# A Mamba layer whose C is broadcast by DMA and copied to PSUM by ScalarE, with pairs of B products in one operation and softplus' correction on ScalarE and TensorE

## The chip, the core and the metric

The kernel runs on one core of a Trainium2 chip, everything in float32. A core has five engines with an instruction queue each, executed in order: TensorE (PE in the profile) for matrix products into PSUM, VectorE (DVE), ScalarE (ACT) for functions of single values, GpSimd (POOL), which reads and writes SBUF only, and SyncE (SP), whose queue here issues DMA transfers. They wait for one another through semaphores. The metric is device time of one execution in microseconds; less is better.

## The reference

Four layers on an image batch x of (2, 128, 56, 56), each `x = x + layer(groupnorm(x))`: agent attention, a 3x3 convolution, a mixture of experts over 2x2 patches, and a pair of Mamba blocks. Only the last one is changed. Its rows are the 112 image rows of 56 points with 128 channels; one Mamba ("f") runs over a row from left to right, the other ("b") from right to left. For each, with inner width 256 and 16 states:

```python
xi, z = jnp.split(x @ in_w.T, 2, axis=-1)
xc = silu(conv_b + sum(xp[:, k:k+L, :] * conv_w[:, k] for k in range(4)))
dt, B, C = split(xc @ xproj_w.T, [8, 8 + 16])
dt = softplus(dt @ dt_w.T + dt_b)
# scan over the 56 points of a row, h of (256, 16):
h = exp(dt * A) * h + (dt * xc) * B
y = (h * C).sum(states)
y = (y + xc * D) * silu(z)
out = y @ out_w.T
```

Both outputs are joined by `fuse_w`, layer-normalized over the channels, and added to x.

## The kernel before, in words

The first three layers fill the time up to about 1710 us; the Mamba layer follows to the end. Each image is cut into 7 blocks of 8 rows, BLK = 448 points, so there are 14 blocks. In a block the two ways follow each other, and a way has 8 pairs of states, each in two units (m = 0 and 1, the two halves of the 256 inner channels): 16 units a way, 32 units a block, 448 in all. A tile of a unit holds 2 states x 64 channels on the 128 partitions and 2 x 448 points along the free axis (the index r takes the other 64 channels of the half).

What one unit needs, with the line in the profile:

- **decay** (L1820): ScalarE writes `dA = exp(dt2 * A)`, two activations of 128x448, into one of two PSUM tiles.
- **push** (L1831): GpSimd multiplies `dtu2` by the pair's row of `Bs` into `dBu`; four buffers.
- **scan** (L1853): VectorE runs the recurrence over 896 points. After the second unit of a pair the 128x1792 tile h is multiplied by C: for the pooled pairs (0, 3, 6 of way f and 0, 3 of way b) by GpSimd from `Cs` (L1859), for the eleven others by VectorE from the PSUM tile `c_ps` (L1862).
- **read_out** (L1841): for those others TensorE writes C into `c_ps`: one row of the low product `lo`, taken with a column of the identity matrix spread over 64 columns, is broadcast to 64 partitions; four matmul instructions a pair.
- **collect** (L1873): TensorE sums h over states into y, some three units behind the scan; **close** (L1879) multiplies y by `zs` on VectorE at a way's end.

What prepares the next way is spread over the units by a hand-written agenda: `book(step, stage)` puts a stage after the unit of that step. A stage mostly issues TensorE's products at once, and its ScalarE part ("fetch") at the next unit, or one later with `late`. The stages: **norm**, **conv** (L1703, L1712), **silu** (two table loads around two Silu), **low** (dt, B and C before their expansion), **send_low** (SP: `lo` to DRAM as `far`, and from there broadcast into `Bs` and, for the pooled pairs alone, into `Cs`), **step** (L1755, L1765 to L1769: dt's product, then |v|, relu(v), e = exp(-|v|) and, back into the PSUM bank, ue = 1 + e), **error** (L1775, VectorE: (ue - 1) - e, the rounding error of ue), **log** (L1780, ScalarE: u = ln(ue)), **softplus** (L1785: TensorE sums u - error + relu over three matrices; L1786 copies dt back), **weigh** (L1793, GpSimd: dt * xc, and a memset of the rows' first points), **send_steps** (L1808, SP: eight transfers that lay dt and dt * xc out as `dt2` and `dtu2`), **gate**. After a block come **fuse**, **measure**, **root**, **newton**, **normalize**, **turn_back** and **onto**.

PSUM is full: two tiles of 1024 for dA, y, one bank under the tag "mm" and one under "c". Stages and `c_ps` share these last two one after the other, so a stage booked with `tag="c"` stands in line with the multiplies by C. All five engines' orders are as the program issues them: for unit n the loop issues decay of unit n + 1, the fetches due, push of unit n + 3, the scan of n, a close that is due, read_out, collects, then the agenda's stages of step n.

Of the kernel before, what the change touches and what calls it, by code (L numbers as in the profile page):

```python
# [17 lines left out]
P = 128  # L18
# [1513 lines left out]
def mamba_pair(net, out, wts, combine):  # L1532
# [19 lines left out]
    with ExitStack() as ctx:  # L1552
# [7 lines left out]
        def gathered(name):  # L1560

            if name == "g0":
                g = work.tile([P, 2, 2, BLK], F32, name=name, tag="h", bufs=4).rearrange("p m r t -> p (m r t)")
            else:
                g = work.tile([P, 2, BLK], F32, name=name, tag="dBu", bufs=4).rearrange("p r t -> p (r t)")
            return g[:T, :512]
# [123 lines left out]
        class Half:  # L1690


            def __init__(self, blk, w):
                self.blk, self.w = blk, w
                self.dA, self.dBu, self.hc = {}, {}, {}
# [20 lines left out]
            def gate(self, m):  # L1716
                pm = mm("gate_ps")
                if m == 0:
                    self.zs = work.tile([P, 2, BLK], F32, name="zs", tag=f"zs{self.w.d}", bufs=1 if self.w.d == "f" else 2)
                nc.tensor.matmul(  # L1720
                    rows(pm[:, :BLK]),
                    self.w.gate[:, m, :],
                    self.blk.xn[:, :, K - 1 : K - 1 + HW],
                    start=True,
                    stop=True,
                )
                return lambda: nc.scalar.copy(self.zs[:, m, :], pm[:, :BLK])
# [9 lines left out]
            def send_low(self):  # L1737

                pooled = self.w.pooled
                far = dram.tile([2 * S, BLK], F32, name="far", tag="far")  # L1740
                nc.sync.dma_start(far, self.lo[R:, :])
                self.B = work.tile([P, PAIRS, BLK], F32, name="Bs", tag="Bs")
                self.C = work.tile([P, len(pooled), BLK], F32, name="Cs", tag=f"Cs{self.w.d}", bufs=1)
                for s in range(2):
# [3 lines left out]
                    for n, j in enumerate(pooled):  # L1748
                        r = S + 2 * j + s
                        nc.sync.dma_start(self.C[half, n, :], far[r : r + 1, :].to_broadcast([H, BLK]))  # L1750


            def step(self, m):
                pm = mm("dt_ps")
                nc.tensor.matmul(pm[:, :BLK], self.w.dt_t[:, m, :], self.lo[:R, :], start=True, stop=True)  # L1755
                if m == 0:
                    self.e = work.tile([P, 2, BLK], F32, name="sp_e", tag="sp_e", bufs=1)
                    self.dt = work.tile([P, 2, BLK], F32, name="dt", tag="dt")
                    self.ue = {}
# [8 lines left out]

# [3 lines left out]

            def error(self, m):
                e = self.e[:, m, :]
                nc.vector.scalar_tensor_tensor(e, self.ue[m], 1.0, e, ALU.subtract, ALU.subtract)  # L1775

            def log(self, m):
                if m == 0:
                    self.u = work.tile([P, 2, BLK], F32, name="sp_u", tag="sp_u", bufs=1)
                nc.scalar.activation(self.u[:, m, :], self.ue[m], AF.Ln)  # L1780

            def softplus(self, m):
                pm = mm("sp_ps")
                for n, (mat, v) in enumerate(((net.ident, self.u), (minus, self.e), (net.ident, self.dt))):
                    nc.tensor.matmul(pm[:, :BLK], mat, v[:, m, :], start=n == 0, stop=n == 2)  # L1785
# [13 lines left out]
            def send_steps(self, m=None):  # L1799

                some = slice(0, 2) if m is None else slice(m, m + 1)
                if not m:
                    self.dt2 = work.tile([P, 2, 2, BLK], F32, name="dt2", tag="dt2")
                    self.dtu2 = work.tile([P, 2, 2, BLK], F32, name="dtu2", tag="dtu2")
# [22 lines left out]
            def push(self, u):  # L1827
                j, m = self.unit(u)
                shape = [P, 2, BLK]
                self.dBu[u] = work.tile(shape, F32, name="dBu", tag="dBu", bufs=4)  # L1830
                nc.gpsimd.tensor_tensor(  # L1831
                    self.dBu[u], self.dtu2[:, m], self.B[:, j, :].unsqueeze(1).to_broadcast(shape), ALU.mult
                )

            def read_out(self, u):

                r = R + S + u // 2 * 2
                self.c_ps = ps.tile([P, 512], F32, name="c_ps", tag="c")
                for s in range(2):
                    one_row = net.ident[:LOW, r + s : r + s + 1].to_broadcast([LOW, H])  # L1840
                    nc.tensor.matmul(self.c_ps[s * H : (s + 1) * H, :BLK], one_row, self.lo, start=True, stop=True)  # L1841

            def scan(self, u):
# [5 lines left out]
                hf, bf = (v.rearrange("p r t -> p (r t)") for v in (h[:, m], self.dBu[u]))  # L1849
# [4 lines left out]
                if m == 1:  # L1854
                    shape = [P, 4, BLK]
                    h4 = h.rearrange("p m r t -> p (m r) t")
                    if self.by_pool(u):
                        c = self.C[:, self.w.pooled.index(j), :].unsqueeze(1).to_broadcast(shape)
# [18 lines left out]
            def close(self):  # L1877
                self.yv = work.tile([P, 2, BLK], F32, name="yv", tag=f"yv{self.w.d}", bufs=1)
# [18 lines left out]
        for n, blk in enumerate(blocks):  # L1897
# [3 lines left out]
            if n == 0:  # L1901
# [9 lines left out]
                for m in range(2):  # L1911
                    book(at + 10 + m, lambda f=f, m=m: f.error(m))
# [9 lines left out]
                for m in range(2):  # L1922
                    book(2 + 3 * m, lambda b=b, m=m: b.step(m))
                    book(3 + 3 * m, lambda b=b, m=m: b.error(m))
# [5 lines left out]
            else:  # L1930
# [11 lines left out]
                book(at + 19, lambda f=f: f.error(0))  # L1942
                book(at + 19, lambda f=f: f.log(0))
                book(at + 20, lambda f=f: f.step(1))
                book(at + 21, lambda f=f: f.error(1))
# [8 lines left out]
                book(at + 28, lambda b=b: b.error(0))  # L1954
                book(at + 28, lambda b=b: b.log(0))
                book(at + 29, lambda b=b: b.step(1))
                book(at + 31, lambda b=b: b.error(1))
# [5 lines left out]
                book(at + 35, lambda b=b: b.gate(0))  # L1963
# [47 lines left out]
        with tc.manual_schedule(engines={E.PE, E.Activation, E.DVE, E.Pool, E.SP}):  # L2011
            units[0][0].decay(0)
            for h, u in units[:3]:
                h.push(u)
            for n, (h, u) in enumerate(units):
# [4 lines left out]
                if n + 3 < len(units):  # L2020
                    who, i = units[n + 3]
                    who.push(i)
# [3 lines left out]
                if u % 2 == 0 and not h.by_pool(u):  # L2026
                    h.read_out(u)
# [115 lines left out]
```

## Time and profile before

| What | us |
|---|---|
| median of 3 runs (lowest, highest) | 3111.37 (3110.33, 3111.38) |
| the profiled execution's own time | 3104.97 |
| its span, first to last instruction | 3103.2 |
| first scan starts, last scan starts | 1736.9, 3073.4 |

| Engine, 1737 to 3070 us (1333 us) | busy us |
|---|---|
| TensorE, matmuls | 1184.50 |
| VectorE | 1247.53 |
| ScalarE | 964.97 |
| GpSimd | 1284.22 |

The profile is one execution. Busy time counts an instruction from start to end, and neighbours on one engine overlap by some tenths of a microsecond, so what an engine can do is read from the distance between starts. A wait is put down to the engine whose semaphore came last. TensorE's clock has two values in the records, full and half; an average clock of 0.89 over a stretch means that it ran at half speed for about a fifth of it.

### The profile page before, as it was taken

How to read it: one execution, taken by the hardware profiler on the slowest of the kernel's cores; microseconds unless marked ns; L12 is line 12 of the kernel's file. 1: busy time of each engine (PE TensorE's matmuls, PEld its weight loads, DVE VectorE, ACT ScalarE, POOL GpSimd, SP SyncE). 2: the span in 40 equal slices, each digit the busy share in tenths (PEclk: the TensorE clock that was granted, in tenths of full speed). 3: DMA queues.
4: the chain of work that ended last, by engine and by line, in shares of the span. 5: the costliest groups of instructions: out<-in, count | busy, mean ns of one | idle time of the engine just before them, and what ended most of it. 6: DMA issues, size and time to landing. Idle time of an engine off the chain costs nothing. (4 is left out here: it accounts for less than half of the span.)

```text
span 3103.2 us, 34608 instructions
## 1 busy us (share of the span) xinstructions
PE 2821.9 (91%) x12964; PEld 1076.6 (35%) x12964; DVE 2224.9 (72%) x2033; ACT 1758.6 (57%) x2634; POOL 1499.1 (48%) x801
## 2 busy tenths in 40 slices
PE   7999999999898899999996789989899998889885
PEld 3333333332334444444443322333323333233321
DVE  5879999999887111111112699999999999999996
ACT  5778788877641011111111577776677767777764
POOL 3000100100511000000003699999999999999995
PEclk9999999999998899999997888999889899999987
DMA  1000000000011878787773553454444535444440
GB/s 54 1 1 1 1 1 1 1 1 1 1 38 43 317 280 323 286 314 301 298 309 104 115 102 81 91 106 90 93 89 84 112 81 113 90 84 91 95 101 8
DMA packets 133271, 333.65 MB, mean 108 GB/s; under 512 B 20228, under 2 KB 90340, under 8 KB 129492
## 3 DMA queue, kind: packets, MB, share of 16 engines
q1 hardware_dynamic: 111104, 303.96, 34.0%
q0 software_dynamic: 5520, 15.62, 1.6%
q10 hardware_dynamic: 16452, 11.61, 1.2%
q8 instruction: 106, 1.74, 0.2%
q14 instruction: 89, 0.73, 0.1%
HBM read 262.56 MB, written 17.20 MB: 90 GB/s over the span
## 5 line engine op out<-in xcount | busy, mean ns | idle before, releaser
L1831 POOL TENSOR_TENSOR dBu<-dtu,Bs 128x896 f32<-128x896 f32 x448 | 943.6, 2136 | 51.7 <-DVE h L1853 39.1
L1853 DVE TENSOR_TENSOR_SCAN h<-dA,dBu 128x896 f32<-128x896 f32 x448 | 878.7, 2006 | 59.7 <-ACT dA L1820 47.4
L620 ACT ACTIVATE ex<-sc 128x896 f32<-128x896 f32 (+1 forms) x700 | 602.7, 917 | 124.4 <-PE sc L617 113.3
L627 DVE TENSOR_TENSOR ex_sum<-ex_sum,ex 128x1792 f32<-128x1792 f32 (+1 forms) x238 | 492.5, 2069 | 35.2 <-ACT ex L620 21.2
L1873 PE MATMUL y<-h,both 128*64 128x448 f32 x1792 | 469.1, 625 | 16.1 <-POOL h L1859 14.9
L617 PE MATMUL sc<-q,k 32*128 32x448 f32 (+1 forms) x2800 | 403.5, 587 | 3.6 <-ACT ex L620 2.9
L1341 PE MATMUL h_ps<-w,xs_c 128*128 128x512 f32 x896 | 393.4, 597 | 10.3 <-issue 10.3
L1820 ACT ACTIVATE dA<-dt,f_A 128x448 f32<-128x448 f32 x448 | 284.4, 637 | 107.0 <-DVE h L1853 76.4
L635 PE MATMUL av<-ex,va 128*32 128x448 f32 (+1 forms) x2800 | 334.3, 552 | 0.1
L1862 DVE TENSOR_TENSOR h<-h,c_ps 128x1792 f32<-128x1792 f32 x154 | 311.3, 2021 | 26.2 <-PE c_ps L1841 11.5
L582 POOL TENSOR_TENSOR a_e<-a_e,a_inv 112x784 f32<-112x784 f32 x14 | 41.6, 2974 | 583.2 <-ACT ex L620 394.5
L1820 ACT ACTIVATE dA<-dt,b_A 128x448 f32<-128x448 f32 x448 | 283.8, 636 | 66.6 <-DVE h L1853 53.2
L1345 DVE TENSOR_TENSOR he<-h_ps,sg 128x512 f32<-128x512 f32 x56 | 38.5, 691 | 381.8 <-PE h_ps L1341 344.3
L1289 POOL DMA_INDIRECT xr<-xd,whom x28 | 28.1, 1003 | 534.8 <-PE xr_ps L1331 490.1
L1859 POOL TENSOR_TENSOR h<-h,Cs 128x1792 f32<-128x1792 f32 x70 | 279.3, 3990 | 2.5 <-DVE h L1853 2.4
L1841 PE MATMUL c_ps<-low,ident 40*64 40x448 f32 x616 | 172.9, 643 | 89.6 <-DVE h L1862 67.5
L1341 PEld LDWEIGHTS h_ps<-w,xs_c 128*128 128x128 f32 x896 | 169.0, 191 | 218.5 <-issue 202.8
L1873 PEld LDWEIGHTS y<-h,both 128*64 128x64 f32 x1792 | 116.7, 150 | 320.0 <-issue 250.7
L617 PEld LDWEIGHTS sc<-q,k 32*128 32x128 f32 (+1 forms) x2800 | 137.7, 181 | 230.0 <-issue 135.2
L1362 PE MATMUL o_ps<-w,ht 128*128 128x512 f32 x448 | 197.2, 592 | 0.4 <-ACT ht L1357 0.4
L1344 ACT ACTIVATE sg<-h_ps 128x512 f32<-128x512 f32 x56 | 33.4, 597 | 256.0 <-PE h_ps L1341 256.0
L1364 ACT ACTIVATE ot<-o_ps,share 128x512 f32<-128x512 f32 x28 | 19.3, 688 | 278.9 <-PE o_ps L1362 278.9
(334 smaller groups left out, 3057.9 us busy)
## 6 DMA issues: line engine op xcount, KB each, us to landing
w<-in_L_conv_w_dram SPq DMA_DIRECT2D x28, 4096.0 KB, 19.4
w<-in_L_conv_w_dram SPq DMA_DIRECT2D x28, 2048.0 KB, 10.2
Bs<-far SPq DMA_DIRECT2D x56, 896.0 KB, 8.6
dtu<-sp_u SPq DMA_DIRECT2D x108, 224.0 KB, 3.9
dt<-dt SPq DMA_DIRECT2D x108, 224.0 KB, 5.2
Cs<-far SPq DMA_DIRECT2D x140, 112.0 KB, 7.3
os<-ot ACTq DMA_DIRECT2D x28, 256.0 KB, 7.8
xd<-xt SPq DMA_DIRECT2D x14, 224.0 KB, 2.7
```

The costliest lines, as they stand in the source:

```text
L617: nc.tensor.matmul(sc[:size, j, :BLK], self.m.k[rows, at : at + size], self.q[rows, :], start=True, stop=True)
L620: nc.scalar.activation(ex[:size, 2 * g : 2 * g + 2, :], sc[:size, :, :BLK], AF.Exp, scale=scale)
L627: nc.vector.tensor_add(self.total[g][:size], self.total[g][:size], ex[:size])
L635: nc.tensor.matmul(self.av[rows, :BLK], self.m.va[:size, i, rows], self.ex[i][:size, h, :], start=i == 0, stop=i == STEPS - 1,)
L1341: nc.tensor.matmul(h_ps, xc[:, q, :], w1[:, q, f0 : f0 + 512], start=q == 0, stop=q == 3)
L1362: nc.tensor.matmul(o_ps, ht[:, i, :], w2[:, i, :], start=i == 0, stop=i == nj - 1)
L1820: nc.scalar.activation(self.dA[u][:, r * BLK : (r + 1) * BLK], self.dt2[:, m, r, :], AF.Exp, scale=self.w.A[:, j, 2 * m + r : 2 * m + r + 1],)
L1831: nc.gpsimd.tensor_tensor(self.dBu[u], self.dtu2[:, m], self.B[:, j, :].unsqueeze(1).to_broadcast(shape), ALU.mult)
L1853: nc.vector.tensor_tensor_scan(hf, af, bf, 0.0, ALU.mult, ALU.add)
L1859: nc.gpsimd.tensor_tensor(h4, h4, c, ALU.mult)
L1862: nc.vector.tensor_tensor(h4, h4, c, ALU.mult)
L1873: nc.tensor.matmul(self.y[r * H : (r + 1) * H, m, :BLK], both, self.hc[j][:, m, r, :], start=False, stop=j == PAIRS - 1)
```

## The change

C now reaches the SBUF for every pair: `send_c` issues two broadcast transfers from `far` a pair, six units ahead, into five buffers. `read_out` becomes a ScalarE copy from there to the PSUM tile and is issued ahead of the scan. `push` makes the products of both units of a pair in one GpSimd operation of 128x1792, two pairs ahead, into three buffers of twice the size. `error` is gone: ScalarE writes ue - 1 into a quarter of `dtu2`, and softplus adds four matrices, e - (ue - 1) + u + relu. `close` writes into `zs`, whose buffers change places (two for f, one for b). A few bookings move.

```diff
             def send_low(self):
-                pooled = self.w.pooled
-                far = dram.tile([2 * S, BLK], F32, name="far", tag="far")
+                far = self.far = dram.tile([2 * S, BLK], F32, name="far", tag="far")
                 nc.sync.dma_start(far, self.lo[R:, :])
                 self.B = work.tile([P, PAIRS, BLK], F32, name="Bs", tag="Bs")
-                self.C = work.tile([P, len(pooled), BLK], F32, name="Cs", tag=f"Cs{self.w.d}", bufs=1)
...
-                    for n, j in enumerate(pooled):
-                        r = S + 2 * j + s
-                        nc.sync.dma_start(self.C[half, n, :], far[r : r + 1, :].to_broadcast([H, BLK]))
+            def send_c(self, j):
+                self.C[j] = work.tile([P, BLK], F32, name="Cs", tag="Cs", bufs=5)
+                for s in range(2):
+                    r = S + 2 * j + s
+                    nc.sync.dma_start(
+                        self.C[j][s * H : (s + 1) * H, :], self.far[r : r + 1, :].to_broadcast([H, BLK])
+                    )
...
-            def error(self, m):
-                e = self.e[:, m, :]
-                nc.vector.scalar_tensor_tensor(e, self.ue[m], 1.0, e, ALU.subtract, ALU.subtract)
             def log(self, m):
...
                 nc.scalar.activation(self.u[:, m, :], self.ue[m], AF.Ln)
+                nc.scalar.activation(self.dtu2[:, m, 0, :], self.ue[m], AF.Identity, bias=-1.0)
             def softplus(self, m):
                 pm = mm("sp_ps")
-                for n, (mat, v) in enumerate(((net.ident, self.u), (minus, self.e), (net.ident, self.dt))):
-                    nc.tensor.matmul(pm[:, :BLK], mat, v[:, m, :], start=n == 0, stop=n == 2)
+                terms = (
+                    (net.ident, self.e[:, m, :]),
+                    (minus, self.dtu2[:, m, 0, :]),
+                    (net.ident, self.u[:, m, :]),
+                    (net.ident, self.dt[:, m, :]),
+                )
+                for n, (mat, v) in enumerate(terms):
+                    nc.tensor.matmul(pm[:, :BLK], mat, v, start=n == 0, stop=n == 3)
...
-            def push(self, u):
-                j, m = self.unit(u)
-                shape = [P, 2, BLK]
-                self.dBu[u] = work.tile(shape, F32, name="dBu", tag="dBu", bufs=4)
+            def push(self, j):
+                shape = [P, 4, BLK]
+                self.dBu[j] = work.tile([P, 2, 2, BLK], F32, name="dBu", tag="dBu", bufs=3)
                 nc.gpsimd.tensor_tensor(
-                    self.dBu[u], self.dtu2[:, m], self.B[:, j, :].unsqueeze(1).to_broadcast(shape), ALU.mult
+                    self.dBu[j].rearrange("p m r t -> p (m r) t"),
+                    self.dtu2.rearrange("p m r t -> p (m r) t"),
+                    self.B[:, j, :].unsqueeze(1).to_broadcast(shape),
+                    ALU.mult,
                 )
             def read_out(self, u):
-                r = R + S + u // 2 * 2
                 self.c_ps = ps.tile([P, 512], F32, name="c_ps", tag="c")
-                for s in range(2):
-                    one_row = net.ident[:LOW, r + s : r + s + 1].to_broadcast([LOW, H])
-                    nc.tensor.matmul(self.c_ps[s * H : (s + 1) * H, :BLK], one_row, self.lo, start=True, stop=True)
+                nc.scalar.copy(self.c_ps[:, :BLK], self.C[u // 2])
...
             def close(self):
-                self.yv = work.tile([P, 2, BLK], F32, name="yv", tag=f"yv{self.w.d}", bufs=1)
+                self.yv = self.zs
...
-                book(at + 28, lambda b=b: b.log(0))
-                book(at + 29, lambda b=b: b.step(1))
-                book(at + 31, lambda b=b: b.error(1))
+                book(at + 29, lambda b=b: b.log(0))
+                book(at + 30, lambda b=b: b.step(1))
                 book(at + 31, lambda b=b: b.log(1))
...
-                book(at + 35, lambda b=b: b.gate(0))
+                book(at + 38, lambda b=b: b.gate(0))
...
+            for h, u in units[:6:2]:
+                h.send_c(u // 2)
             units[0][0].decay(0)
-            for h, u in units[:3]:
-                h.push(u)
+            for h, u in units[:4:2]:
+                h.push(u // 2)
             for n, (h, u) in enumerate(units):
...
                 fetch(n)
-                if n + 3 < len(units):
-                    who, i = units[n + 3]
-                    who.push(i)
+                if u % 2 == 0 and not h.by_pool(u):
+                    h.read_out(u)
+                if u % 2 == 0 and n + 6 < len(units):
+                    who, i = units[n + 6]
+                    who.send_c(i // 2)
+                if n % 2 == 0 and n + 4 < len(units):
+                    who, i = units[n + 4]
+                    who.push(i // 2)
                 h.scan(u)
                 if done:
                     done.pop().close()
-                if u % 2 == 0 and not h.by_pool(u):
-                    h.read_out(u)
                 waiting.append((h, u))
```

Tiles that were written to a `dBu` buffer during the gather before the layer take the new shape, and `dtu2` is made in `step` instead of `send_steps`; all other bookings of `error` are taken out.

## Prediction

> **What bounds the kernel now.** The change lies in the Mamba layer, from the first scan at 1736.9 us to the last at 3073.4. I read the groups of instructions first, for who is full there: the page's groups (line, engine, operation, shapes, count | busy us, mean ns | idle).
>
> ```profile
> L1831 POOL TENSOR_TENSOR dBu<-dtu,Bs 128x896 f32<-128x896 f32 x448 | 943.6, 2136 | 51.7 <-DVE h L1853 39.1
> L1853 DVE TENSOR_TENSOR_SCAN h<-dA,dBu 128x896 f32<-128x896 f32 x448 | 878.7, 2006 | 59.7 <-ACT dA L1820 47.4
> ...
> L1862 DVE TENSOR_TENSOR h<-h,c_ps 128x1792 f32<-128x1792 f32 x154 | 311.3, 2021 | 26.2 <-PE c_ps L1841 11.5
> ...
> L1859 POOL TENSOR_TENSOR h<-h,Cs 128x1792 f32<-128x1792 f32 x70 | 279.3, 3990 | 2.5 <-DVE h L1853 2.4
> ```
>
> VectorE and GpSimd are both nearly full. Who holds whom is in the waits of 1900 to 3060 us, 12 blocks (waiter <- releaser: us, times, longest):
>
> ```profile
> ACT sp_u L1780 <- DMA dtu<-sp_u: 44.9, 12, 4.4
> DVE h L1853 <- ACT dA L1820: 38.8, 35, 2.0
> ...
> ACT dt L1786 <- PE sp_ps L1785: 37.2, 25, 2.5
> ...
> POOL dBu L1831 <- DVE h L1853: 29.3, 34, 1.9
> ...
> DVE h L1862 <- PE c_ps L1841: 5.2, 12, 0.9
> ```
>
> The scan waits for ScalarE's dA, never to speak of for GpSimd's dBu, while GpSimd waits for scans to free its buffers. So the layer's pace is VectorE's own work plus the holes that ScalarE's in-order queue tears in it; GpSimd, however full, follows. The holes of one block, in the timeline of VectorE (start, length, ... [idle before <- releaser]):
>
> ```profile
> 2315.90 3.94 DVE L1853 TENSOR_TENSOR_SCAN h<-dA,dBu 128x896 f32<-128x896 f32 x2 [1.11 <-ACT dA L1820]
> ...
> 2330.89 2.02 DVE L1862 TENSOR_TENSOR h<-h,c_ps 128x1792 f32<-128x1792 f32 x1 [0.66 <-PE c_ps L1841]
> ...
> 2358.25 7.77 DVE L1853 TENSOR_TENSOR_SCAN h<-dA,dBu 128x896 f32<-128x896 f32 x4 [0.84 <-ACT dA L1820]
> ...
> 2378.86 0.61 DVE L1775 SCALAR_TENSOR_TENSOR sp_e<-dt_ps,sp_e 128x448 f32<-128x448 f32 x1
> 2381.46 3.94 DVE L1853 TENSOR_TENSOR_SCAN h<-dA,dBu 128x896 f32<-128x896 f32 x2 [1.98 <-ACT dA L1820]
> ```
>
> A block of 32 units: a scan run of four takes 7.76, so 1.92 from start to start; a pair read out on VectorE is 1.92 + 2.10 + 1.94 = 5.96, a pooled one 3.85; 11 x 5.96 + 5 x 3.85 = 84.8; two yv at 1.0, the layer norm's small operations 1.8, four corrections (L1775) at 0.53 start to start: 90.7. Holes 0.5 (mean) + 0.43 + 0.84 + 1.98 = 3.7. Sum 94.4; measured 95.0 (scans of unit 0 at 2322.42 and seven blocks later at 2987.37). GpSimd in a block: 32 x 2.10 + 5 x 3.96 + 5.5 = 92.5.
>
> **The change, part by part.** Sums are made against the profiled execution, 3105.0 us (span 3103.2); it lies 6.4 under the median 3111.4, which I add at the end.
>
> *B products of a pair.* 16 operations of 128x1792 for 32 of 128x896. The multiply by C on L1859 has exactly that shape and kind: 3.96 start to start. 16 x 3.96 = 63.4 against 67.2: GpSimd -3.8 a block, to 88.7. As the scan hardly waits for it this is worth 0; its upper bound, if GpSimd set the pace, is 3.8 x 14 = 53 us. Behind it: after weigh at step 25 only one push (3.96) stands before the next way's first, where three (6.3) stood; that push waited 0.92 for its data at 2314.20, and will wait some 3.3. It still ends about 3 us ahead of its scan. Cost 0, bound 2.4 a block.
>
> *The correction leaves VectorE.* Four STT at 0.53 go: -2.1 a block. But the first, at 2378.86, lies in the hole before 2381.46, so only 1.6 shortens the path. In its place: four ScalarE Identity of 128x448 and a fourth matrix for TensorE, by these groups of 1780 us to the end:
>
> ```profile
> L1785 PE MATMUL sp_ps<-sp_e,minus 128*128 128x448 f32 x104 | 47.6, 539 | 0.0
> ...
> L1775 DVE SCALAR_TENSOR_TENSOR sp_e<-dt_ps,sp_e 128x448 f32<-128x448 f32 x52 | 31.9, 612 | 2.6 <-ACT dt_ps L1769 2.1
> ...
> L1769 ACT ACTIVATE dt_ps<-sp_e 128x448 f32<-128x448 f32 x52 | 28.5, 548 | 1.6
> ```
>
> ScalarE pays about 0.45 each, start to start. The matrix adds 0.82 (three took 2291.95 to 2294.41).
>
> *C on ScalarE.* The one-row matmuls (four of 0.24, 0.97 a pair, 11 pairs) leave TensorE, -10 a block, on an engine that bounds nothing: 0 by itself. ScalarE gets 11 copies at 0.45 (the rows L1769 and, for a copy, L1735's 0.524): 5 a block, with the Identities 6.8 on 69 busy of 95. A copy waits until VectorE's multiply of the pair before has left the bank; behind it wait that step's ScalarE stages and the next dA.
>
> *Hole by hole, ScalarE's queue walked in its new order.*
> Step 18 (silu): from 2368.06, the end of VectorE's multiply, the old chain is low product and copy 2.2, dA 1.25, ln 0.6, dA 1.25, four softplus operations 2.2, two table loads and two Silu 4.4, dA 1.4: 13.3. VectorE has 7.9 + 1.94 + 1.0 + 0.53 = 11.4: hence the 1.98. The new copy stands before the Silu (+0.45) and the correction is gone from under it (0.53): hole 3.0, +1.0.
>
> ```profile
> 2375.65 1.28 ACT L1884 ACT_TABLE_LOAD   x1
> ...
> 2380.05 1.31 ACT L1820 ACTIVATE dA<-dt,b_A 128x448 f32<-128x448 f32 x2
> ```
>
> Right after it the Identity pushes dA(21) 0.44 back, against 0.3 of slack: +0.2.
> Steps 32 to 35: both softplus sums go through the c bank, and the C of the pair behind them needs that bank too. Old: from 2322.61 sum, copy, collect and gate, sum, copy, C by TensorE, 8.3 to the multiply at 2330.89. New: 2 x 0.82 more for the fourth matrices, 0.65 less for a copy than for TensorE's C: 9.3, from the end of the previous multiply at which the bank comes free, against 7.8 of scans: hole 1.65, +1.2. This holds if TensorE runs at full speed there.
> Steps 28 to 30: log moves behind a dA, so the DMA that it waits for (44.9 over 12 blocks) no longer delays that dA; hole 0.5 to 0.2: -0.3.
> Step 10: the second convolution's result comes a little earlier without C's matmuls, then a copy of 0.45: 0.84 to 0.55, -0.3. The moved gate (steps 35 to 38; one product of 1.03, a copy of 0.53) puts the first convolution behind its copy, by 0.2, inside a wait of 0.64: 0.
>
> *TensorE's speed.* The trace shows two speeds:
>
> ```profile
> 2374.20 0.97 PE L1873 MATMUL y<-h,both 128*64 128x448 f32 x4
> 2378.00 1.76 PE L1841 MATMUL c_ps<-low,ident 40*64 40x448 f32 x4 [2.82 <-DVE h L1862]
> ```
>
> Four products in 0.97, and after an idle 2.82 in 1.76, for some 6 us. With C's matmuls gone TensorE idles more, most around steps 28 to 31, just ahead of the two sums. Half speed until it has been busy for two stretches of 3.4 us (2315.6 to 2322.4 in this block) costs the sums 0 to 3.2; I take 1.0, nearer to the full-speed row, since the sum of four full matrices keeps the array busy longer.
> The Trainium skill, "TensorE: Matmul & The Clock Gate", part 1, says that the clock is halved after an idle window of about 3.4 us and restored after a busy one. The trace halves it after an idle 2.82 already. By that page alone the 1.0 would be 0.
> The Trainium skill, "ScalarE: Activation LUTs", Rules for kernel authors, speaks against the move: it sends add and mul to VectorE, as faster. Here the rows give 612 ns on VectorE and 548 on ScalarE, so the operation itself is no dearer; by the page the four Identities would cost more than my 0.45, and the sum would be higher.
>
> *SP.* 32 C transfers a block instead of 10, at 0.63 an issue: +14, of SP's idle time. They queue behind send_steps, which waits for GpSimd's memset about 20 us each time:
>
> ```profile
> SPq L1808 <- POOL dt L1797: 469.8, 24, 24.2
> ```
>
> Worst place: send_steps is issued 2306.87 to 2313.2, C for unit 34 then by 2314.5, landing after 7.3 (the page's median) at 2321.8; ScalarE wants it near 2326. Covered, by 4 us; if DMA traffic eats that, each late microsecond is one of VectorE. Cost 0, bounds 0 to 2 a block. B tiles go on the same queue ahead of C twice a block, with 8 us to spare.
>
> *Ends.* Before the first scan the push of a pair ends 1.85 later, the sums 1 to 2 later; scan 2 then waited 1.2 and absorbs much: +1. Last block, nothing prepared beside it: GpSimd's two waits of 0.5 go: -1. yv kept in zs changes no instruction.
>
> *Sum.* The four corrections and the holes (step 18's +1.0 holds the 0.53 that saves nothing): -2.1 + 1.0 + 0.2 + 1.2 + 1.0 - 0.3 - 0.3 = +0.7 a block; 13 blocks +9; ends 0. 3105 + 9 = 3114 profiled, **3121 at the median**. The bounds of TensorE's speed (-1.0, +2.2) and of SP give 3107 to 3150.
>
> **The rivals.**
> *ScalarE has room, so VectorE keeps its 2.1* (faster). For it: ScalarE is idle for 25 of 95 us. The holes stay as they are: 14 x 2.1 = 29, 3082; with GpSimd's relief shortening log's wait too, another 1 a block, 3068. Against it: two of four holes are chains that the edits lengthen. It decides if the two added chains come out under 1.4 together instead of 3.2.
> *TensorE slow through the sums* (slower): with 10 us less work a block it drops to half speed also for the low product and both ways' sums: +3.2 at steps 32 to 35 and +1.5 at step 18 instead of 1.0: +4.4 a block, 3168.
> *C late* (slower): the transfers land after ScalarE asks, 2 us a block: 3147.
> *Nothing gained or lost*: holes up by what the correction frees, 3111.
>
> **How the numbers follow.** A measurement of this kernel tells about 0.2%, 6.2 us, from no change. Forecast 0.45, of which 0.08 lies within 6.2; ScalarE has room 0.28; TensorE slow 0.14; C late 0.05; nothing 0.08. Faster 0.28, same 0.16, slower 0.56. Range 3076 to 3158: below it lies the deeper form of the first rival, above it most of the slow TensorE. The forecast's own range is 3107 to 3150.
>
> **What would show it.** dBu 224 operations near 3.99 us, GpSimd under 90 of 95; the scan's wait for dA above 38.8; a hole near 3 before the scan after the second Silu; the multiply's wait, now for ScalarE's copy, near 1.7 or more after b's softplus; ScalarE's dt copy waiting longer than 37.2 for sp_ps. Wrong, if the scan's wait for dA falls, if scans wait for dBu, or if a Cs transfer releases ScalarE.

## The result and the profile after

The changed kernel took 3160.81 us (median; 3159.17 to 3167.06) beside 3110.85 for the kernel before on the same chip: a ratio of 1.0165, 95% interval 1.0147 to 1.0182, slower by about 50 us. Its profiled execution took 3160.94 us (span 3159.2) where that of before took 3104.97 (3103.2). The forecast was 3121 with a range up to 3158: the sign was right, the time lies 40 us above the forecast and just outside the range.

The groups of the page (line, engine, operation, shapes, count | busy us, mean ns | idle ahead):

```profile
L1856 DVE TENSOR_TENSOR_SCAN h<-dA,dBu 128x896 f32<-128x896 f32 x448 | 882.1, 2008 | 95.4 <-ACT dA L1824 76.0
L1834 POOL TENSOR_TENSOR dBu<-dtu,Bs 128x1792 f32<-128x1792 f32 x224 | 912.8, 4097 | 63.6 <-DMA dtu<-sp_u 34.2
...
L1865 DVE TENSOR_TENSOR h<-h,c_ps 128x1792 f32<-128x1792 f32 x154 | 311.3, 2021 | 51.1 <-ACT c_ps L1844 37.2
...
L1862 POOL TENSOR_TENSOR h<-h,Cs 128x1792 f32<-128x1792 f32 x70 | 278.8, 3983 | 69.5 <-DVE h L1856 69.0
```

VectorE's operations cost what they did; only the idle ahead of them grew (59.7 to 95.4 ahead of the scans, 26.2 to 51.1 ahead of the multiplies by C). GpSimd got its relief, 912.8 us for 943.6, and waits more. The waits of 1900 to 3110 us, 12 blocks (waiter <- releaser: us, times, longest):

```profile
PE y L1872 <- DVE zs L1882: 105.7, 25, 6.7
ACT dt L1791 <- PE sp_ps L1790: 72.1, 32, 3.1
DVE h L1856 <- ACT dA L1824: 62.9, 44, 2.8
DVE h L1865 <- ACT c_ps L1844: 27.8, 24, 2.2
...
POOL dBu L1834 <- DVE h L1856: 15.5, 15, 2.3
```

TensorE's skip products (xc times D, the first products of a new y) wait 105.7 us for the closing of the y before, a wait that the kernel before does not show. ScalarE's copy of dt waits for the softplus sums nearly twice as long (37.2 before), and the multiply by C now waits for ScalarE (5.2 for TensorE before). In the timeline of VectorE in one block (start, length, ..., [idle before <- releaser]) the holes stand at new places:

```profile
2355.19 2.02 DVE L1865 TENSOR_TENSOR h<-h,c_ps 128x1792 f32<-128x1792 f32 x1 [1.34 <-ACT c_ps L1844]
...
2366.97 0.87 DVE L1641 BATCH_NORM_STATS2 ln_st<-ln_y 112x6 f32<-112x128 f32 x4 [0.86 <-ACT ln_y L1635]
...
2370.64 0.16 DVE L1657 SCALAR_TENSOR_TENSOR ln_t<-ln_mv,ln_ps 112x4 f32<-112x4 f32 x1 [0.61 <-ACT ln_ps L1649]
...
2384.83 7.77 DVE L1856 TENSOR_TENSOR_SCAN h<-dA,dBu 128x896 f32<-128x896 f32 x4 [1.44 <-ACT dA L1824]
...
2399.15 3.94 DVE L1856 TENSOR_TENSOR_SCAN h<-dA,dBu 128x896 f32<-128x896 f32 x2 [0.58 <-issue]
2403.51 2.02 DVE L1865 TENSOR_TENSOR h<-h,c_ps 128x1792 f32<-128x1792 f32 x1 [0.42 <-ACT c_ps L1844]
...
2409.30 4.05 DVE L1856 TENSOR_TENSOR_SCAN h<-dA,dBu 128x896 f32<-128x896 f32 x2 [2.77 <-ACT dA L1824]
```

Summed by the step at which they stand, and taken as means over 12 blocks of the two timelines, these holes give a ledger that can be laid beside the prediction's:

| Step of the block | before, us | after, us | measured change | predicted |
|---|---|---|---|---|
| 1 | 0 | 0.34 | +0.34 | 0 |
| 3 (behind b's softplus sums) | 0.48 | 2.32 | +1.84 | +1.2 and +1.0 |
| 6, 7 (layer norm) | 0 | 1.56 | +1.56 | 0 |
| 12 | 0.81 | 1.43 | +0.62 | -0.3 |
| 18, 19 (low product, C) | 0 | 1.45 | +1.45 | 0 |
| 20, 21 (behind the second Silu) | 2.20 | 2.77 | +0.57 | +1.0 and +0.2 |
| 30 | 0.56 | 0 | -0.56 | -0.3 |
| four corrections gone | | | -2.1 | -2.1 |
| sum | | | +3.7 | +0.7 |

From the first scan to the last it is 1388.6 us where it was 1336.5, 52 more. The first block did not grow (107.0 us after 107.5); the twelve of the table grew by 4.1 each, of which these holes account for 3.7.

TensorE shows where the holes of steps 6 and 7 come from. The products of a new way's skip term, in the kernel before and then in the kernel after (timeline of TensorE):

```profile
2331.68 1.03 PE L1720 MATMUL gate_ps<-pad,b_gate_t 128*128 128x448 f32 x2
2332.97 0.97 PE L1841 MATMUL c_ps<-low,ident 40*64 40x448 f32 x4 [0.26 <-DVE h L1862]
2333.97 1.77 PE L1869 MATMUL y<-xc,f_skip 128*128 128x448 f32 x4
2335.67 0.97 PE L1873 MATMUL y<-h,both 128*64 128x448 f32 x4
```

```profile
2358.26 2.81 PE L1872 MATMUL y<-xc,f_skip 128*128 128x448 f32 x4 [3.35 <-DVE zs L1882]
2361.01 1.57 PE L1876 MATMUL y<-h,both 128*64 128x448 f32 x4
...
2392.94 1.76 PE L1876 MATMUL y<-h,both 128*64 128x448 f32 x4 [2.97 <-POOL h L1862]
2394.87 2.05 PE L1732 MATMUL low_ps<-xc,f_xp_t 128*40 128x448 f32 x3 [0.18 <-DVE h L1865]
```

Before, the gate's product and C's two matmul groups stood right ahead of the skip products and TensorE was at full speed. After, it idles 3.35 us and the same products take 1.6 us more; the fuse products behind them, ScalarE's copy of the fused rows and VectorE's layer norm are late with them. Further on it idles 2.97 for GpSimd's h, and the product low is slow (2.05 us for three instructions).

### The profile page after: what moved, and what is told of

Same layout as the page of the kernel before. It is cut to its first block, busy times and chain, and to the rows that moved or that the text cites. A ratio compares the mean times of both kernels' runs of the same rounds, so it can differ in the third digit from the quotient of the medians.

```text
span 3159.2 us, 34042 instructions
## 1 busy us (share of the span) xinstructions
PE 2747.3 (87%) x12460; PEld 1084.8 (34%) x12460; DVE 2200.6 (70%) x1977; ACT 1847.4 (58%) x2844; POOL 1470.0 (47%) x577
## 5 line engine op out<-in xcount | busy, mean ns | idle before, releaser
L1856 DVE TENSOR_TENSOR_SCAN h<-dA,dBu 128x896 f32<-128x896 f32 x448 | 882.1, 2008 | 95.4 <-ACT dA L1824 76.0
L1834 POOL TENSOR_TENSOR dBu<-dtu,Bs 128x1792 f32<-128x1792 f32 x224 | 912.8, 4097 | 63.6 <-DMA dtu<-sp_u 34.2
L1876 PE MATMUL y<-h,both 128*64 128x448 f32 x1792 | 479.5, 623 | 66.5 <-POOL h L1862 51.4
L1865 DVE TENSOR_TENSOR h<-h,c_ps 128x1792 f32<-128x1792 f32 x154 | 311.3, 2021 | 51.1 <-ACT c_ps L1844 37.2
L625 DVE TENSOR_TENSOR ex_sum<-ex 128x1792 f32<-128x1792 f32 x56 | 114.4, 2043 | 54.6 <-ACT ex L620 54.5
```

The source lines that it names most:

```text
L1834: nc.gpsimd.tensor_tensor(self.dBu[j].rearrange("p m r t -> p (m r) t"), self.dtu2.rearrange("p m r t -> p (m r) t"), self.B[:, j, :].unsq ...
L1856: nc.vector.tensor_tensor_scan(hf, af, bf, 0.0, ALU.mult, ALU.add)
L1865: nc.vector.tensor_tensor(h4, h4, c, ALU.mult)
L1876: nc.tensor.matmul(self.y[r * H : (r + 1) * H, m, :BLK], both, self.hc[j][:, m, r, :], start=False, stop=j == PAIRS - 1)
```

## The experiments

Two theories stood against each other. *Speed*: TensorE, with less to do, falls to half speed after idle stretches, and what it then makes late is a step of VectorE's. *Line*: ScalarE's longer queue, and the bank "c" in which two longer sums and C's copy follow one another, are late at whatever speed.

**The parts alone.** Each kernel is the one before with one part of the change; `only_zs` is the closing into `zs` and the gate's move, `only_pair` has the pairs besides. Kernels without the part on C send the pooled pairs' C by `send_c` all the same, and `dtu2` is made in `step`; `zs_fill` below has both of these too, at 1.0015.

```diff
 only_zs, against before:
-                book(at + 35, lambda b=b: b.gate(0))
+                book(at + 38, lambda b=b: b.gate(0))
-                self.yv = work.tile([P, 2, BLK], F32, name="yv", tag=f"yv{self.w.d}", bufs=1)
+                self.yv = self.zs
```

C alone: 

> The kernel before with one part of the change alone: C by DMA for every pair and ScalarE's copies into the c bank, ahead of the scan. The theory that TensorE, without C's products, idles, falls to half speed and hands that on through ScalarE's in-order queue expects most of the loss here: holes of VectorE at step 6 (the layer norm's statistics waiting for ln_y) and step 18, about 0.9 us each a block, beside 0.5 for a copy in the queue at steps 19 and 20: 2.5 to 3.5 us a block, 3143 to 3160 in all. The rival, that only the longer ScalarE queue counts, expects no hole at step 6 and none above 0.5 at step 18, 1 to 1.5 a block: 3122 to 3132.

Softplus' correction alone: 

> The kernel before with softplus' correction on ScalarE and TensorE alone, and its moved log and step. Both theories: VectorE saves 2.1 us a block, the hole before the multiply at step 3 grows by two matrices, 1.6, and that at step 20 by 0.5: about 0 a block, 3105 to 3118. If half speed through the sums matters even while TensorE keeps C's products, 3125 or more.

Pairs, closing and gate: 

> The kernel before with the products of a pair in one GpSimd operation, and yv in zs (its space is needed), with the gate moved to step 38. GpSimd bounds nothing, so the pair gives 0; the gate's copy ahead of root costs VectorE 0.6 us at step 7, and half a microsecond at step 12 through the first convolution: 3115 to 3125. If GpSimd's relief shortens the wait of log for dtu's transfer (hole 0.56 at step 30), 3108 to 3118. If GpSimd set the pace: under 3100.

Closing and gate: 

> The kernel before with yv in zs alone, which moves the first gate product of way b from step 35 to 38; C stays on TensorE, products per unit, the correction on VectorE. Theory now: that product kept TensorE from idling ahead of y's first products and fuse at steps 2 to 4; without it TensorE idles there, drops to half speed, fuse comes late, and VectorE's statistics wait at step 6; so the move alone costs all that the pair kernel lost: 3145 to 3158. Rival: the pair of products did it, by holding back a pooled h or dtu's push: 3108 to 3118 here.

| Kernel | ratio to before | interval |
|---|---|---|
| only_c | 1.0017 | 0.9999 to 1.0036 |
| only_sp | 1.0116 | 1.0090 to 1.0143 |
| only_pair | 1.0151 | 1.0126 to 1.0177 |
| only_zs | 1.0144 | 1.0127 to 1.0161 |

C costs next to nothing by itself, less than either of its expectations: the granted clock falls (0.937 to 0.924 on average), but no hole opens at step 6 save in one block. `only_pair` came out above all of its expectations, yet the pairs cost nothing (`only_pair` less `only_zs`). Two parts cost: the correction 36 us, and the gate moved by three steps 45 us, which the prediction had put at 0. Together they would be over 80 us, but the whole change costs 50: they share a loss.

The correction's own 36 us are only in part explained. Its holes stand at step 1 (1.66 a block), at step 3 (3.11 where the kernel before has 0.48) and at step 27 (0.88). Half speed has a share: way b's first sum takes 3.3 to 4.7 us there, 3.3 being full speed.

**The moved gate.** The timelines of VectorE and TensorE of `only_zs`:

```profile
2365.79 0.87 DVE L1641 BATCH_NORM_STATS2 ln_st<-ln_y 112x6 f32<-112x128 f32 x4 [2.17 <-ACT ln_y L1635]
```

```profile
2354.77 1.76 PE L1842 MATMUL c_ps<-low,ident 40*64 40x448 f32 x4 [1.22 <-DVE h L1863]
2356.46 3.35 PE L1870 MATMUL y<-xc,f_skip 128*128 128x448 f32 x4
2359.74 1.66 PE L1874 MATMUL y<-h,both 128*64 128x448 f32 x4
```

The four skip instructions take 3.35 us instead of 1.77. If that is what costs, a product that nobody reads, put where the gate's product was, must give the time back although ScalarE's queue stays as it is:

```diff
 zs_fill, against only_zs (idle_gate: the gate's product into a tile of the mm bank, no copy):
+                book(at + 35, b.idle_gate)
                 book(at + 38, lambda b=b: b.gate(0))
```

> The kernel before with yv in zs and the gate moved, as in the run that did this alone (3153), and in the gate's old place at step 35 the same product into the mm bank, read by nobody. TensorE's queue up to fuse is then the one of before. If TensorE idling there, and its half speed, makes the loss: the hole at step 6 (2.17) goes and most of the additional 1.1 at step 12; the 0.6 at step 7 stays: 0.6 to 1.2 us a block over the kernel before, 3116 to 3124. If the loss comes from ScalarE's copy ahead of root, or from the shared zs buffers: 3145 to 3158.

Ratio 1.0015, interval 1.0005 to 1.0025: 40 of the 45 us are back. The timeline of TensorE, with the added product in its first line:

```profile
2424.02 1.03 PE L1731 MATMUL idle_ps<-pad,b_gate_t 128*128 128x448 f32 x2
2425.31 0.97 PE L1852 MATMUL c_ps<-low,ident 40*64 40x448 f32 x4 [0.26 <-DVE h L1873]
2426.31 1.77 PE L1880 MATMUL y<-xc,f_skip 128*128 128x448 f32 x4
```

VectorE's 2.17 ahead of the layer norm is gone (no idle stands before that line), while a hole of 1.9 at step 12 is in both. So nearly all of the gate's loss is TensorE's speed, shown by taking the cause away and leaving the move.

The same product in the changed kernel, the gate put later still, and both:

```diff
 fill3, against after:
+                book(at + 35, b.idle_gate)
 gate43, against after:
-                book(at + 38, lambda b=b: b.gate(0))
+                book(at + 43, lambda b=b: b.gate(0))
```

> The changed kernel with one more matrix product at step 35, where the gate's was: the same product into the mm bank, read by nobody. If half speed makes fuse late: the hole at step 6 (0.95) goes, and part of that at step 12: 1 to 1.6 us a block, 3138 to 3150. If it is the order of ScalarE's queue: nothing, 3158 to 3168, for TensorE only has one product more.

> The changed kernel with way b's first gate product at step 43 instead of 38, behind both convolutions of way f. Both theories: the copy no longer stands ahead of root, so the hole at step 7 (0.61) goes, and the convolutions come earlier, half of the 1.43 at step 12: 1.2 a block, 3142 to 3150; the hole at step 6 stays, or grows by 0.5 where TensorE has one product less to do.

> Both edits on the changed kernel. If TensorE's speed and the queue order are independent: 2.3 to 2.8 us a block, 3122 to 3132. If only the order counts: as the gate at 43 alone, 3142 to 3150.

Ratios 1.0166 (1.0149 to 1.0183), 1.0159 (1.0142 to 1.0176) and 1.0166 (1.0149 to 1.0183): no help. In the timeline of `fill3` the added product itself came too late:

```profile
2355.23 1.03 PE L1731 MATMUL idle_ps<-pad,b_gate_t 128*128 128x448 f32 x2 [1.99 <-ACT zs L1727]
2356.58 2.81 PE L1882 MATMUL y<-xc,f_skip 128*128 128x448 f32 x4 [0.32 <-DVE zs L1892]
```

It waited for the mm bank, which way f's gate held until ScalarE, itself held up by the softplus sums, had copied it. With the gate at 43 the hole of step 7 went and one of 2.66 at step 15 came. In the whole change something earlier is late first.

**The two softplus sums.** `c_sp` is the changed kernel without pairs, without the closing into `zs`, and with the gate back at step 35.

> The changed kernel without the pairs of products and without yv in zs: the gate's product is back at step 35, GpSimd multiplies per unit. If the moved gate makes most of what the prediction missed: holes at steps 6 and 7 gone and that at step 12 near 0.8, 2 us a block less than the changed kernel: 3128 to 3138. If the parts simply add up, 5 for C and 37 for softplus alone: 3145 to 3152.

Ratio 1.0185, interval 1.0161 to 1.0209, as slow as the whole change and outside both expectations: gate and pairs add nothing to the other two parts. Nor does the gate's product at its old place save the skip products here. It comes late, as in `fill3`, and they run at half speed behind it (timeline of TensorE); the hole of step 6 is 0.85 a block, 0.95 in the changed kernel:

```profile
2354.89 1.03 PE L1720 MATMUL gate_ps<-pad,b_gate_t 128*128 128x448 f32 x2 [1.99 <-ACT zs L1727]
2356.24 3.09 PE L1870 MATMUL y<-xc,f_skip 128*128 128x448 f32 x4 [0.32 <-DVE yv L1880]
```

`c_sp_mm` takes the second sum of way b out of the c bank, and `sp_mm` does the same to `only_sp`:

```diff
 c_sp_mm, against c_sp:
+                book(at + 32, lambda b=b: b.softplus(1), late=1)
-                book(at + 33, lambda b=b: b.softplus(1), tag="c")
```

> As the last one, and way b's second softplus sum goes into the mm bank at step 32, right behind the first, its copy one unit later; the c bank is then free for C a sum earlier. If the two sums in one bank make the hole at step 3: it goes (1.75 and 0.57 a block in the changed kernel), 2 us a block less than the last one: 3098 to 3112. If TensorE's half speed at the sums makes it: 0.5 less.

> The kernel before with softplus' correction alone (3142 to 3145), and the second sum in the mm bank at step 32. One bank for two sums as the cause: the holes at step 3 (2.55 and 0.56 a block) go down to under 0.6, 3106 to 3118. Else, with ScalarE's two Identities ahead of dA as the cause, the hole at step 1 (1.66) stays and the time is above 3130.

`c_sp_mm`: 1.0034 (1.0020 to 1.0049), 47 of 57 us back with one booking. `sp_mm`: 1.0074 (1.0054 to 1.0094) after 1.0116; a third of that loss. Its hole at step 1 stays (1.32 a block), as expected if ScalarE's Identities ahead of dA make it; they were not tested by themselves. The new booking does away with the line, but it also lets eight matrices run in one go, so it doesn't tell speed from line. Products of zeros into the open sum y do, since they keep TensorE busy and leave every booking and bank alone:

```diff
 c_sp_fill2, against c_sp (c_sp_fill: 8 and 6 instead of 5 and 2):
+            def fill(self, count):
+                some = net.ident[:, :112].unsqueeze(1).to_broadcast([P, 4, 112])
+                for _ in range(count):
+                    out = self.y[:, 0, :BLK].rearrange("p (a t) -> p a t", a=4)
+                    nc.tensor.matmul(out, net.zero.to_broadcast([P, P]), some, start=False, stop=False)
...
+                if n > STEPS:
+                    who.fill({30: 5, 31: 2}.get(n % STEPS, 0))
                 run(n)
```

> C and softplus' correction moved, pairs and gate as before, both sums in the c bank, and added products of zeros into the open sum y: eight ahead of the stage of step 30 and six at step 31, some 0.48 us each, where TensorE idled 4.37 and 1.23 us. If half speed in the sums is the cause of its 3163: 3115 to 3130, with the first sum's matrices at 0.91 us for two instructions instead of 1.70. If the line of sum, copy, sum, copy, C in one bank costs whatever the speed: 3150 to 3165; in between if both do.

> As c_sp_fill, with five products of zeros instead of eight ahead of the stage of step 30 and two instead of six at step 31: a product took 0.79 us there, so that fourteen were 11 us and ended 2.5 us after the multiply that frees the bank, ahead of the sums. Now they end before it. If half speed in the first sum is what makes the line in the c bank late: 3115 to 3130, the hole at step 3 (3.95 a block in c_sp_fill) under 1.0. If the line itself is too long at either speed: 3145 to 3165, that hole 2 to 4.

`c_sp_fill`, 1.0141 (1.0125 to 1.0158), decided nothing: a product of zeros took 0.79 us, not the 0.48 that I had allowed, and the fourteen ended 2.6 us after the bank was free, ahead of the sums. `c_sp_fill2`, with seven: 1.0056 (1.0036 to 1.0075), 40 of the 57 us back. The sums in the timelines of TensorE, of `c_sp` and then of `c_sp_fill2`:

```profile
2341.46 1.86 PE L1790 MATMUL sp_ps<-sp_e,ident 128*128 128x448 f32 x2 [1.23 <-DVE h L1863]
2343.11 1.70 PE L1790 MATMUL sp_ps<-dtu,minus 128*128 128x448 f32 x2
2344.61 1.70 PE L1790 MATMUL sp_ps<-sp_u,ident 128*128 128x448 f32 x2
2346.10 1.02 PE L1790 MATMUL sp_ps<-dt,ident 128*128 128x448 f32 x2
```

```profile
2433.83 1.02 PE L1792 MATMUL sp_ps<-sp_e,ident 128*128 128x448 f32 x2 [1.25 <-DVE h L1865]
2434.69 0.92 PE L1792 MATMUL sp_ps<-dtu,minus 128*128 128x448 f32 x2
2435.44 0.92 PE L1792 MATMUL sp_ps<-sp_u,ident 128*128 128x448 f32 x2
2436.19 0.91 PE L1792 MATMUL sp_ps<-dt,ident 128*128 128x448 f32 x2
```

The wait for the bank ahead of both is the same, and the sum takes 5.7 us in the one and 3.3 in the other. This is what VectorE's multiply behind them waits, in `c_sp` and in `c_sp_fill2` (where a hole of 1.14 ahead of a scan has gone besides):

```profile
2353.16 2.02 DVE L1863 TENSOR_TENSOR h<-h,c_ps 128x1792 f32<-128x1792 f32 x1 [2.14 <-ACT c_ps L1842]
```

```profile
2443.15 2.02 DVE L1865 TENSOR_TENSOR h<-h,c_ps 128x1792 f32<-128x1792 f32 x1 [0.90 <-ACT c_ps L1844]
```

So speed is the larger part, and the line the rest: with the sums at full speed the multiply still waits 0.9 in this block and 1.26 on average (under 1.0 was expected), and in `c_sp_mm`, without the line, not at all. Either repair gives most of the loss back. The profiled execution of `c_sp_mm` is the fastest of its six (3103.38 us, median 3118.47), so its holes are those of a good execution. In it half of the blocks still have a sum at half speed; the hole that these leave, ahead of a scan of step 3, is 0.5 a block on average, where `c_sp` has 1.2 there and 2.0 at the multiply.

An earlier attempt to keep TensorE busy, in the changed kernel, failed as an experiment. It put products of C's size, in pieces, into 64 unused columns of the c bank:

```diff
 warm, against after (idle_products: 14 products of 40x64 by 64 columns a pair, never read):
+                if u % 2 == 0 and not h.by_pool(u):
+                    h.idle_products(u)
```

> The changed kernel with TensorE given back as much work as C's products were, at the same place in its queue, into the 64 unused columns of the c bank; nothing reads it, ScalarE's copies stay. If TensorE's half speed makes the unforeseen part of the loss: the holes at steps 6 and 18 (0.95 each) go and that at step 3 shrinks by up to 0.6, 2 to 2.5 us a block: 3128 to 3138. If the length of ScalarE's queue makes it: no gain, 3155 to 3170, as TensorE has only more to do.

Ratio 1.1162 (1.1132 to 1.1191): VectorE's multiply waited for them, 218.7 us in all by the page, since they share C's tile. It tells nothing of the theories, only that a filler must not stand in the line that it is to relieve.

**The whole change with two banks.** `after_mm` is the changed kernel with the booking of `c_sp_mm`; `after_mm_idle` has the unread gate product besides.

> The whole change, with way b's second softplus sum in the mm bank (booked at step 32, fetched one unit later) instead of behind the first in the c bank. Theory A (the moved gate's product is a loss of its own, 45 us alone, and adds to what is left of C and softplus): 3150 to 3162, holes at steps 6, 7 and 12 as after the change. Theory B (the parts overlap; one loss, that of the two sums in one bank, holds most of it): 3115 to 3128.

> The same, with a second, unread gate product on TensorE at step 35, where the gate stood before it was moved. Theory A with the speed of TensorE as its cause: 3112 to 3128, the hole at step 6 gone, the skip product of the next way at 1.77 us for four instructions instead of 2.81 or 3.35. If the place of the gate's copy on ScalarE's queue is what costs: as the run without the unread product, 3150 or more.

1.0038 (1.0026 to 1.0050) and 1.0035 (1.0023 to 1.0047): the parts overlap. Pairs, closing and moved gate cost nothing that can be measured once the sums are early (1.0034 without them). TensorE then comes to the skip products at full speed in ten of thirteen blocks, as the timeline of `after_mm` shows in one:

```profile
2437.39 0.97 PE L1876 MATMUL y<-h,both 128*64 128x448 f32 x4
2438.29 1.04 PE L1720 MATMUL gate_ps<-pad,f_gate_t 128*128 128x448 f32 x2
2439.26 0.97 PE L1876 MATMUL y<-h,both 128*64 128x448 f32 x4
2442.43 1.77 PE L1872 MATMUL y<-xc,f_skip 128*128 128x448 f32 x4 [2.20 <-DVE zs L1882]
```

**What was left, and a version that is no slower.** `c_sp_mm_fill` puts six products of zeros behind the gate's product of step 14, where TensorE waited about 3.2 us for GpSimd's h; `best` moves way f's step(0) behind the second Silu.

```diff
 c_sp_mm_fill, against c_sp_mm:
                 run(n)
+                if n > STEPS:
+                    who.fill({14: 6}.get(n % STEPS, 0))
 best, against c_sp_mm_fill:
-                book(at + 17, lambda f=f: f.step(0))
+                book(at + 18, lambda f=f: f.step(0))
```

> The two sums in two banks (3118 before), and six products of zeros into y behind the gate's product of step 14, where TensorE waits 3.2 us for GpSimd's h and then runs the low product slowly. If that slowness makes the holes at steps 18 and 19 (1.03 and 0.44 a block): 3098 to 3108, faster than the kernel before by 0 to 0.4%. If these holes come from ScalarE's longer queue: 3115 to 3122.

> As c_sp_mm_fill, with way f's step(0) booked at 18 instead of 17, so that its four ScalarE operations (2.2 us) stand behind the two Silu and their table loads instead of ahead of them. If the hole at step 20 (2.77) is ScalarE's queue alone, it falls to some 0.6, and up to 1.5 of it comes back at step 21: 0.7 to 2 us a block, 3080 to 3097. If the time only moves to the next dA: 3103 to 3108.

`c_sp_mm_fill`: 0.9984 (0.9974 to 0.9995), from 1.0034. Half speed had been at work there too (the low product 1.29 us for three instructions and not 1.99). The hole at step 18 fell from 1.03 to 0.60 us a block, that at step 19 stayed at 0.42; what is left there may be ScalarE's queue, which was not tested. It is the fastest kernel here, but 0.16% is less than the 0.2% that a measurement of this kernel tells from no change. `best`: 0.9991 (0.9979 to 1.0002). The time only moved: 0.97 at step 20 and 2.36 at step 21 for 2.77 and none.

## Why the prediction was wrong

**The pace.** It was read rightly. VectorE with the holes in it sets the time, GpSimd follows; the pairs, a third of the change, are worth 0 (1.0151 with them, 1.0144 without), and no wait of a scan for dBu stands among the waits of 1900 to 3110 us. C was not late either: no Cs transfer released ScalarE, and C alone is 1.0017.

**Right terms.** Step 20 at 3.0 (2.77 measured), the hole behind b's sums at 2.65 (2.32), step 30 to about nothing, the four corrections. The working of steps 32 to 35 gave 9.3 us from the bank's release to the multiply, at full speed; in the block shown above, whose sums ran at full speed, the multiply of the pair before ended at 2345.81 and the next began at 2355.19, 9.4 later. (9.3 less the 7.8 of scans is 1.5; the prediction wrote 1.65.) TensorE's term of 1.0 came true at the place where it was put: in the changed kernel every other block has way b's first sum at half speed (5.4 us for 3.3); in such blocks the multiply waits 2.2 and a scan ahead of it mostly 1.1, in the others 1.3 and 0, so half speed costs about 1.0 on the mean over the blocks.

**The step that failed: what TensorE's lost work covers, put at 0.** The prediction priced half speed at one place, the two sums, and put the rest of TensorE's losses at nothing: C's products "0 by itself", the moved gate 0. Half speed struck three places. The skip and fuse products were the second (steps 6 and 7, +1.56 a block with the idle 3.35 ahead of them), the low product the third (a part of the +1.45 at steps 18 and 19; `c_sp_mm_fill` gave 0.43 of it back). I had costed both at 0; at step 18 I walked ScalarE's queue with the old length of the low product.

The moved gate shows the error by itself. I walked ScalarE's queue past it and found a wait that covers the copy. I did not ask what stood on TensorE in its old place: the copy is near 0 indeed (all that is left in `zs_fill` is some 5 us), and the product was worth 40 us alone. In the whole change it is not a loss to be added: `c_sp` has the gate at its old place and is no faster. There the loss starts earlier, at the sums and their one bank, and one booking at that place gave back 39 of the 50 us. C alone was rightly put near 0 (1.0017); together with the longer sums it costs more: 57 us in `c_sp`, 5 and 36 for its two parts.

**Step 12**, forecast to shrink by 0.3, grew by 0.62; the gate's move alone takes it to 1.9, with or without the unread product, so it is not the speed at the skip products. The gate's place has a share of it: the hole is 1.43 in the changed kernel, 1.05 with the gate behind both convolutions (`gate43`) and 1.04 with it at 35 (`c_sp`); with two banks it is 1.43 with the gate at 38 (`after_mm`) and 0.41 with it at 35 (`c_sp_mm`). The hole of 0.34 at step 1 (1.66 in `only_sp`) was not walked at all: ahead of that scan's dA stand the four operations, the logarithm and the Identity of way b's second step.

**The range.** It took the bounds of TensorE's speed and of SP one at a time; both together would have given 3121 + 13 x 4.2 = 3176, and 3161 inside it. That would have been luck, for SP cost nothing.

**The rival nearest to the result** was "TensorE slow through the sums", 3168, to which I gave 0.14. Its time is near, its terms are not: it asked 3.2 at the sums, where half speed cost about 1.0, had its 1.5 at step 18 right by luck (1.45, of which 0.43 is shown to be speed), and had nothing at steps 6, 7 and 12. The trace of before showed half speed after an idle 2.82, and the change removes work from that engine in two parts of four; with this the rival had deserved more than "ScalarE has room", which the walk of the holes already spoke against.

## What to carry to other kernels

Before taking work from an engine that bounds nothing, look at what its neighbours in time are: on TensorE here, a product of 1 us ahead of a chain was worth 3 us a block, whether anybody read it or not. When parts of a change cost more alone than together, look for one stretch that all of them make late, and repair that; here one booking, a second bank for the second of two sums, gave back 39 of 50 us. A filler that tests such a cause must be sized by its own measured duration and must not share a tile with the work that it is to help.

## What the runs showed of the hardware

TensorE's half speed does not follow from the idle stretch alone. The skip products ran at full speed behind an idle 2.20 in `after_mm`, and at half speed in `only_zs`, where the C group ahead of them had been slow since an idle 1.22. In the changed kernel the same idle of 3.35 us was followed in alternate blocks by first instructions of 0.64 us and of 1.1 us; from the fourth to the last but one, its blocks alternate between 97.4 and 100.6 us, within 0.2. The Trainium skill, "TensorE: Matmul & The Clock Gate", Part 1, says that activity is watched in a free-running window of about 3.4 us, and that idle must last such a window. The alternation agrees with a window that runs freely of the kernel; the half speed behind 1.22 us does not agree with the length. In the stretches of `only_zs` around it (start and end, length, busy TensorE, its weight loads, VectorE, ScalarE and GpSimd with their instructions, granted clock, share and GB/s of the DMA) TensorE is busy for 1.99 of the 3.41 us ahead of the drop:

```profile
2347.51:2350.93 3.42, 3.42 (x10) 1.43 (x8) 3.42 (x3) 1.84 (x4) 3.42 (x2) 1.00 0.57 144
2350.93:2354.34 3.41, 1.99 (x9) 0.39 (x8) 2.79 (x2) 3.18 (x6) 3.41 (x2) 1.00 1.04 207
2354.34:2357.75 3.41, 2.98 (x6) 1.13 (x7) 3.41 (x4) 0.24 (x2) 3.41 (x3) 0.50 1.07 198
2357.75:2361.17 3.42, 3.42 (x7) 0.63 (x5) 3.32 (x2) 2.48 (x4) 3.42 (x3) 0.50 0.55 123
2361.17:2364.58 3.41, 3.41 (x31) 3.25 (x30) 2.45 (x2) 0.00 (x0) 3.41 (x2) 1.00 0.00 0
```

So a stretch that is idle for less than half of it can be followed by half speed; how much work is enough stays open.

Between the first and the last scan, each stretch at one granted clock lasts a whole number of these 3.41 us (3.413 in the traces' record of the clock), in every trace here. The blocks of several kernels settle on the same measure. Those of `only_zs`, `only_pair` and `gate43` take some 99.0 us, 29 times 3.413; the alternating two of the changed kernel and of `fill3` take 198.0 together, 58 times; the later ones of `zs_fill` some 95.6, 28 times; the kernel before, at 94.5 to 96.7, keeps to none. In such a kernel a hole that goes can be taken up by another, as in `gate43`. This may be why the losses of the parts do not add up and why `fill3` and `gate43` changed nothing; no run tests it.

One GpSimd multiply of 128x1792 took 4.10 us where two of 128x896 took 4.27: joining them saved 0.17 us a pair by these means, where the prediction's distances between starts had given 0.24.
